# Swapping which tiles' products run on GpSimd in a selective-scan kernel, and moving its GpSimd calls, sums and side-stream steps between slots

## The chip, the cores and the metric

The kernel runs on one core of one Trainium2 chip. The metric is device time in microseconds (us) of one execution, given as the median of several. The core has TensorE (PE in the profile), VectorE (DVE), ScalarE (ACT), GpSimd (POOL) and SyncE (SP, which here issues all DMAs of the loop). Each engine works through its own queue in program order and waits on semaphores.

## The reference

Two layers on `x` of shape (8, 96, 64, 64), float32. Layer 0 is a vision state-space block with a four-direction selective scan, followed by a channel-attention convolution block; layer 1 is linear attention and an FFN with emulated float8 rounding. Cut to what matters:

```python
# layer 0, per image b of 8; C=96, DI=192 inner channels, N=16 states, 4 directions k, l = 4096 positions
xz = einsum('bhwc,ec->bhwe', layernorm(x), in_proj_w);  xw, z = split(xz)
xc = silu(depthwise_conv3x3(xw) + conv_b)
xs = [s0, s1, s0 reversed, s1 reversed]              # 8x8 windows, row- and column-first
dts, B, C = split(x_proj_w @ xs);  delta = softplus(dt_w @ dts + dt_b);  A = -exp(A_logs)
for t in range(l):                                    # for every k, channel d, state n
    h = exp(delta[t] * A) * h + (delta[t] * u[t]) * B[t]
    y[t] = sum_n h * C[t]
y = layernorm(sum of the 4 directions + D * u) * silu(z)
x1 = x * skip_scale + y @ out_proj
hcab = conv3x3(gelu(conv3x3(layernorm(x1))));  x = x1 * skip_scale2 + hcab * gate(mean(hcab))
# layer 1, on tokens t of 96 channels
t = t + linear_attention(layernorm(t));  t = t + ffn_with_float8_rounding(layernorm(t))
```

## The kernel before

**Units, tiles, slots.** The scan is cut into 256 units, written by one loop: 8 images, 4 directions, 8 chunks of 512 positions. A unit has 6 tiles (two halves `g` of the states, times three groups `j` of 64 channels); a tile is 4 slots, so a unit has 24 slots. One slot is one 128x512 scan instruction on VectorE: 64 channels times 2 states on the partitions, 512 positions along the row.

**One tile.** `inputs` (GpSimd, one 128x2048 multiply, line 1001) makes `hb` = delta*u*B for the four slots. `decays` (ScalarE, line 1129) writes exp(delta*A) of the slot two ahead into `da`, a PSUM buffer of four banks. The scan (VectorE, line 1204) runs the recurrence. Then comes the product with C: for a "banked" slot the scan writes over `da`, and VectorE multiplies `da` by C into `hb` one slot later (`product`, line 1210); otherwise the scan writes over `hb`, and GpSimd multiplies in place, four slots at once (`outputs`, line 1009). `BANKED` gives for each tile how many of its 4 slots are banked. Line 1211 or 1216 (ScalarE) copies the last column into `carry` for the next chunk. `sums` (TensorE, line 1029) adds states and halves into PSUM tiles `p`, and `gather` (ScalarE, lines 1051 and 1054) evicts them.

**The order around it** is written by hand. `plan` puts calls into the slots of a unit; the main loop emits, for each slot, the carry copies that were kept, the decay two ahead, the scan, the product of the slot before, the planned calls, and one step of the side streams. In `plan`, `u` is the unit itself, `last` the one before, `nxt` and `third` the ones after. `inputs` is put two tiles ahead into 6 buffers (`HB`). `states` loads B and C, 1 MB each for half a unit, into two buffers each; `spread` loads delta and delta*u by channel group; `scaled_input` (GpSimd, line 983) makes delta*u; `step_sizes` (ScalarE, softplus between two table loads) stands in slot 9.

**Side streams.** Generators interleave the front end of the next image (`front`) and the back end of the last (`back_end`) with the scan. A `yield n` is n slots; `yield PA` (2 slots) stands after matmuls whose result the next step reads. The steps on VectorE are at lines 302, 450, 465, 476, 545, 597, 614, 648 and 653. Each waits in VectorE's queue, between two scans, if TensorE or ScalarE is not yet done. In `gated`, ScalarE's square (line 449) and VectorE's multiply (line 450) read the same PSUM bank `dy`, in this order. `norm` is the shared layer norm, whose last step is ScalarE's `inv_std` (lines 246 and 247). `quiet` holds silu and gelu, each between two table loads (line 275), until the slot is in `CALM`. `landed` holds a step until a number of slots has passed since its DMA's request. SyncE issues every DMA of the loop; `later` gives a DMA to it three slots after the request.

Of the kernel before, what the change touches and what calls it, by code (L numbers as in the profile page):

```python
# [12 lines left out]
AF = mybir.ActivationFunctionType  # L13
# [6 lines left out]
B, C, HW = 8, 96, 64  # L20
# [10 lines left out]
SPREAD = 5  # L31
HB = 6

BANKED = ((4, 0, 4, 0, 4, 3), (4, 0, 4, 0, 4, 4))

HOLD = 3
LAND = 11
# [1 line left out]
PA = 2  # L39
# [4 lines left out]
def kernel(ctx: ExitStack, tc: tile.TileContext, a, out):  # L44
# [8 lines left out]
    nc = tc.nc  # L53
# [105 lines left out]
    def landed(*parts):  # L159
        while clock[0] < max(p.ready for p in parts):  # L160
            yield 1
# [56 lines left out]
    def windowed(ap):  # L218

        return ap.rearrange("p (w i j) -> p i w j", w=8, i=8)  # L220

    def raster(ap):
        return ap.rearrange("p (i w j) -> p i w j", i=8, w=8)

    def square(ap):
        return ap.rearrange("p (r w) -> p r w", r=8)
# [22 lines left out]
    def norm(k, srcs, sq, d):  # L249

        ps = bank(k.tag, "ctr")[:C, :]
        for i, src in enumerate(srcs):
            nc.tensor.matmul(ps, cen_c, src, start=i == 0, stop=i == len(srcs) - 1)  # L253
        yield PA
        nc.scalar.activation(sq, ps, AF.Square)
        nc.scalar.copy(d, ps)  # L256
        yield 1
        ps = bank(k.tag, "var")[:C, :]
        nc.tensor.matmul(ps, ones_c, sq, start=True, stop=True)  # L259
        yield PA  # L260
        inv_std(ps, ps)
        yield 1
        return ps

    alone = [False]
    place = [None]
    CALM = (0, 1, 16, 17)

    def quiet():

# [135 lines left out]
    def back_end(b, s):  # L406
# [8 lines left out]
        def gated(k, cs):  # L415


            def fetch_y(c):
                fetch(k.ya, s["y"][0][0:P, bass.ts(c, T)])
                fetch(k.yb, s["y"][0][P:DY, bass.ts(c, T)])  # L420

            def fetch_z(c):
                fetch(k.za, s["zd"][0:P, bass.ts(c, T)])
                fetch(k.zb, s["zd"][P:DI, bass.ts(c, T)])

            def fetch_base(c):
                fetch(k.bs, s["base"][:, bass.ts(c, T)])

            bs, r = k.bs.t[:C], k.r[:C]
            full, low, up, early = slice(0, P), slice(0, 64), slice(64, P), 0  # L430
            for n, c in enumerate(cs):
                while c not in s["done"]:
                    yield 1
                if n == 0 or early < n:
                    fetch_y(c)
                if n == 0:
                    fetch_z(c)
                    fetch_base(c)
                after = cs[n + 1] if n + 1 < len(cs) else None
                yield from landed(k.ya, k.yb, k.za, k.zb, k.bs)  # L440
                for rows, (wa, wb_), z, sq in (
                    (full, (cen_aa, cen_x), k.za.t, k.s1),
                    (up, (cen_x[:, 0:64], cen_bb), k.zb.t, k.s2[up]),
                ):
                    ps = bank(k.tag, "dy")[rows, :]
                    nc.tensor.matmul(ps, wa, k.ya.t, start=True, stop=False)  # L446
                    nc.tensor.matmul(ps, wb_, k.yb.t, start=False, stop=True)  # L447
                    yield PA
                    nc.scalar.activation(raster(sq), windowed(ps), AF.Square)
                    nc.vector.tensor_tensor(raster(z), windowed(ps), raster(z), ALU.mult)  # L450
                    yield 1
                if after in s["done"]:
                    fetch_y(after)
                    early = n + 1
                ps = bank(k.tag, "var")[:C, :]
                nc.tensor.matmul(ps, cen_x[:, 0:C], k.s1, start=True, stop=False)
                nc.tensor.matmul(ps, cen_x[up, 0:C], k.s2[up], start=False, stop=True)
                yield PA
                inv_std(r, ps, -1.0)
                yield 1  # L460
                ps = bank(k.tag, "attn")[:C, :]
                nc.tensor.matmul(ps, wy[0], k.za.t, start=True, stop=False)
                nc.tensor.matmul(ps, wy[1][up], k.zb.t, start=False, stop=True)
                yield PA
                nc.vector.tensor_tensor(r, ps, r, ALU.mult)
                if after is not None:
                    fetch_z(after)
                later(x1d[:, bass.ts(c, T)], r)
                if early == n and after in s["done"]:
                    fetch_y(after)  # L470
                    early = n + 1
                yield 1
                rs = yield from norm(k, (r, bs), k.s1[:C], k.d1[:C])
                if after is not None:
                    fetch_base(after)
                nc.vector.tensor_tensor(k.pad[0:C, :, 1 : HW + 1], square(k.d1[:C]), square(rs), ALU.mult)
                if early == n and after in s["done"]:
                    fetch_y(after)
                    early = n + 1
                later(xld[:C, 1 + 8 * c : 9 + 8 * c, :], k.pad)  # L480
                if k.solo and n == 5:
                    fetch_rows(k.im, xld, NC - 2)
                yield 1
# [42 lines left out]
        def second_conv(k, cs):  # L526
            if not k.solo:
                for p, c in zip(k.m3, cs):
                    nearer(p, c)
            for n, c in enumerate(cs):  # L530
                yield from landed(k.m3[n % 2])
                ps = bank(k.tag, "cab2")[:C, :]
                for dx in range(3):
                    nc.tensor.matmul(  # L534
                        ps, cab2_w[:, dx, :], k.m3[n % 2].t[:, :, dx : dx + HW], start=dx == 0, stop=dx == 2
                    )
                    if dx == 1:
                        yield 1
                yield PA
                if n + 2 < len(cs):  # L540
                    nearer(k.m3[n % 2], cs[n + 2])
                t = (k.s1, k.d1)[n % 2][:C]
                nc.scalar.activation(t, ps, AF.Identity, bias=cab2_b)  # L543
                yield 1
                nc.vector.tensor_reduce(totals[:, c : c + 1], t, AX.X, ALU.add)
                later(td[:, bass.ts(c, T)], t)
                if n == len(cs) - 1:
                    sources(k, cs[0])
                yield 1
# [29 lines left out]
        def attention(k, cs):  # L579

            t, x1, bs, new = k.ya.t[:C], k.za.t[:C], k.bs.t[:C], k.r[:C]
            for n, c in enumerate(cs):
                yield from landed(k.ya, k.za, k.bs)
                ps = bank(k.tag, "x2")[:C, :]
# [10 lines left out]
                rs = yield from norm(k, (new,), k.s1[:C], k.d1[:C])  # L595
# [4 lines left out]
                ps = bank(k.tag, "lnt")  # L600
# [8 lines left out]
                ps = bank(k.tag, "gram")[: C + 1, : C + 1]  # L609
                for i in range(4):  # L610
                    part = lnt[:, i * (C + 1) : (i + 1) * (C + 1)]
                    nc.tensor.matmul(ps, part, part, start=i == 0, stop=i == 3)  # L612
                yield PA
                nc.vector.tensor_tensor(gram, ps, gram, ALU.add)
                if n == len(cs) - 1:
                    normed_again(k, 0, cs[0])
# [23 lines left out]
        def feed_forward(k, cs):  # L640

            for n, c in enumerate(cs):
                t = k.t2[n % 2].t[:C]
                yield from landed(k.ln, k.t2[n % 2])
                ps = bank(k.tag, "att")[:C, :]
                nc.tensor.matmul(ps, small["qkvf"], k.ln.t, start=True, stop=True)
                yield PA
                nc.vector.scalar_tensor_tensor(t, ps, bff, t, ALU.add, ALU.add)  # L648
                if n + 1 < len(cs):
                    normed_again(k, n + 1, cs[n + 1])  # L650
# [1 line left out]
                rs = yield from norm(k, (t,), k.s1[:C], k.d1[:C])  # L652
                nc.vector.tensor_tensor(k.x8, k.d1[:C], rs, ALU.mult, saturate=False)  # L653
                yield 1
                for f in range(3):
                    ps = bank(k.tag, "ff1")
# [16 lines left out]
                ps = bank(k.tag, "ff2")[:C, :]  # L673
# [60 lines left out]
    for b in range(out.shape[0]):  # L734
# [3 lines left out]
        for order, (pair, back) in enumerate((p, k) for p in s["pairs"] for k in range(2)):  # L738
            for i in range(NC):
                u = Unit()  # L740
# [321 lines left out]
    def plan(u, last, nxt, third, fourth):  # L1062
# [3 lines left out]
        def put(slot, f, *args):  # L1066
            at[slot].append((f, args))

        if last:
            put(0, outputs, last, 5)  # L1070
            for m in range(2):
                put(m, sums, last, (3, 4), 2 + m)
            for m in range(2):
                put(3 + m, sums, last, (5,), m)
            put(3, gather, last, 0)
            put(7, states, u, 1, 1)
            put(7, gather, last, 1)
        for n in range(6):
            to = (u, n + 2) if n < 4 else (nxt, n - 4)
            if to[0]:  # L1080
                put(4 * n + 1, inputs, *to)
        if third and u.i % 2:
            put(16, scaled_input, (nxt, third))
        put(8, outputs, u, 1)
        put(16, outputs, u, 3)
        for m in range(4):
            put(13 + m, sums, u, (0, 1), m)
            if m < 2:
                put(18 + m, sums, u, (2,), m)
                put(22 + m, sums, u, (3, 4), m)  # L1090
        put(18, before, u)
        if nxt:
            put(0, spread, nxt, 0, (0, 1))
# [69 lines left out]
    for u in units:  # L1163
# [29 lines left out]
        for slot in range(24):  # L1193
            n, m = divmod(slot, G)
# [30 lines left out]
    for f in kept:  # L1225
        f()
    outputs(u, 5)
    for m in range(2):
        sums(u, (3, 4), 2 + m)
    for m in range(2):  # L1230
        sums(u, (5,), m)
    gather(u, 0)
# [79 lines left out]
```

## Time and profile before

| | us |
|---|---|
| median of 3 runs | 10794.53 (10794.46 to 10806.23) |
| the profiled execution's own time | 10803.4 |
| its span | 10801.7 |
| VectorE busy | 10015.9 (93%) |
| GpSimd busy | 9994.5 (93%) |
| TensorE busy | 8566.6 (79%) |
| ScalarE busy | 7636.8 (71%) |
| mean share of the DMA queue's packets | 84.8% |
| 6144 scans (line 1204), mean of the commonest form | 1.273 |
| 3890 products on VectorE (line 1210), mean | 0.668 |
| 1536 `inputs` (line 1001), mean | 4.546 |
| 512 full `outputs` (line 1009), mean | 4.535 |
| 384 `scaled_input` (line 983), mean | 1.29 |

Instructions of VectorE and of GpSimd overlap a little at their ends, so that the next one starts earlier than the mean duration says: on VectorE 1.18 us after a scan's start and 0.59 us after a product's, on GpSimd 4.48 us after a 128x2048 multiply's. The scans run from 179.0 to 10569.1 us of the span; before lies the setup and the front end of image 0, behind it the end of image 7. A unit takes 40.6 us on the mean.

### The profile page before, as it was taken

Reading aid. Unit: us, or ns where it says so; the run is one execution under the profiler, and the core shown is the slowest. Engines: PE = TensorE matmul, PEld = TensorE weight load, DVE = VectorE, ACT = ScalarE, POOL = GpSimd, SP = SyncE. Lnnn points to the kernel's source line nnn. Section 1 sums busy time; section 2 is a strip of 40 time slices with the busy share of each in tenths; the row PEclk is TensorE's granted clock in tenths of the full one; section 3 lists DMA queues with packets and bytes.
Section 4 is the critical chain, followed back from the end, with each engine's and each line's share of the span. In section 5 each row is a group of like instructions: output and inputs, shape, how many; then the busy total and the mean of one; then the engine's idle time right before and its main releaser. Section 6 shows DMA issues by size and latency. Waiting matters only on the chain. (4 is left out here: it accounts for less than half of the span.)

```text
span 10801.7 us, 96773 instructions
## 1 busy us (share of the span) xinstructions
PE 8566.6 (79%) x23270; PEld 2293.4 (21%) x23270; DVE 10015.9 (93%) x10848; ACT 7636.8 (71%) x14954; POOL 9994.5 (93%) x2732
## 2 busy tenths in 40 slices
PE   7777768886788868888688886888778887777677
PEld 2121112221122212222122221222212221111122
DVE  3999999999999999999999999999999999999993
ACT  4666666777677776777777777677776777666674
POOL 3999998999999999999999999999998999999991
PEclk8787778987788878888789887888878987788788
DMA  6888888988889878898888988899888988888883
GB/s 148 205 206 212 200 211 210 228 222 202 216 212 225 224 195 222 210 230 216 201 215 211 237 209 204 212 219 232 201 214 213 220 228 201 204 204 210 210 211 93
DMA packets 1095373, 2253.23 MB, mean 209 GB/s; under 512 B 435993, under 2 KB 436698, under 8 KB 963731
## 3 DMA queue, kind: packets, MB, share of 16 engines
q1 hardware_dynamic: 1094803, 2247.05, 84.8%
q8 instruction: 185, 3.03, 0.1%
q14 instruction: 385, 3.15, 0.1%
HBM read 1507.14 MB, written 336.69 MB: 171 GB/s over the span
## 5 line engine op out<-in xcount | busy, mean ns | idle before, releaser
L1001 POOL TENSOR_TENSOR hb<-b,du 128x2048 f32<-128x2048 f32 x1536 | 6949.6, 4546 | 23.9 <-PE p L1029 16.8
L1129 ACT ACTIVATE da<-delta,w_a_logs 128x512 f32<-128x512 f32 x6144 | 4147.6, 689 | 496.6 <-DVE hb L1204 400.4
L1029 PE MATMUL p<-hb,halves 128*64 128x512 f32 x12288 | 3786.8, 706 | 791.0 <-POOL hb L1009 630.7
L1204 DVE TENSOR_TENSOR_SCAN da<-da,carry,hb 128x512 f32<-128x512 f32 x3385 | 4258.5, 1273 | 129.5 <-ACT carry L1211 55.9
L1009 POOL TENSOR_TENSOR hb<-hb,c 128x2048 f32<-128x2048 f32 (+1 forms) x718 | 2587.7, 3604 | 395.5 <-ACT carry L1216 373.6
L1210 DVE TENSOR_TENSOR hb<-da,c 128x512 f32<-128x512 f32 x3890 | 2599.3, 668 | 1.8 <-DMA c<-xd 0.8
L1204 DVE TENSOR_TENSOR_SCAN hb<-da,carry,hb 128x512 f32<-128x512 f32 x1991 | 2451.4, 1264 | 65.2 <-ACT carry L1211 49.2
L1211 ACT COPY carry<-da 128x1 f32<-128x1 f32 x3890 | 609.9, 157 | 1784.0 <-DVE hb L1210 1775.1
L1029 PEld LDWEIGHTS p<-hb,halves 128*64 128x64 f32 x12288 | 907.4, 157 | 3551.9 <-issue 1979.6
L313 PE MATMUL conv<-f0im,taps 97*128 97x512 f32 (+1 forms) x2088 | 890.2, 675 | 45.9 <-ACT f0pre L369 42.4
L275 ACT ACT_TABLE_LOAD x705 | 904.5, 1283 | 13.7 <-PEq L1301 0.8
L1204 DVE TENSOR_TENSOR_SCAN da<-da,hb 128x512 f32<-128x512 f32 x505 | 605.3, 1214 | 56.4 <-POOL hb L1001 54.0
L962 PE MATMUL dt<-dts,dt_w 7*128 7x512 f32 (+1 forms) x1024 | 484.9, 740 | 157.0 <-ACT yt L1054 69.1
L983 POOL TENSOR_TENSOR ua<-nat,ua 128x512 f32<-128x512 f32 x256 | 329.8, 1288 | 167.0 <-DMA ub<-u 157.9
L313 PEld LDWEIGHTS conv<-f0im,taps 97*128 97x128 f32 (+1 forms) x2088 | 257.9, 177 | 629.3 <-issue 532.2
L1216 ACT COPY carry<-hb 128x4 f32<-128x4 f32 (+1 forms) x718 | 140.1, 195 | 323.5 <-DVE hb L1204 318.5
L1204 DVE TENSOR_TENSOR_SCAN hb<-da,hb 128x512 f32<-128x512 f32 x263 | 308.1, 1205 | 3.4 <-ACT carry L1211 2.1
L259 PE MATMUL var<-f1e,ones_c 96*96 96x512 f32 x350 | 215.8, 701 | 119.5 <-ACT f1e L256 63.4
L253 PE MATMUL ctr<-f1e,cen_c 96*96 96x512 f32 x402 | 226.7, 672 | 105.0 <-DVE f1e L648 43.1
L657 PE MATMUL ff<-f1x,q_w 96*128 96x512 fp8e5 x174 | 83.0, 477 | 254.2 <-DVE f1x L653 150.9
L497 PE MATMUL cab<-f1im,cab_w 97*32 97x512 f32 x1044 | 261.5, 615 | 13.4 <-DMA f1im<-xld 7.2
L534 PE MATMUL cab<-f1m,cab_w 96*96 96x512 f32 x348 | 213.8, 735 | 54.4 <-ACT f1e L543 25.8
(427 smaller groups left out, 7118.3 us busy)
## 6 DMA issues: line engine op xcount, KB each, us to landing
b<-xd SPq DMA_DIRECT2D x1024, 512.0 KB
c<-xd SPq DMA_DIRECT2D x1024, 512.0 KB
delta<-nat SPq DMA_DIRECT2D x1536, 128.0 KB
du<-ua SPq DMA_DIRECT2D x1024, 128.0 KB
y<-yt SPq DMA_DIRECT2D x512, 256.0 KB
u<-y SPq DMA_DIRECT2D x384, 256.0 KB
ua<-u SPq DMA_DIRECT2D x256, 256.0 KB
du<-ub SPq DMA_DIRECT2D x512, 128.0 KB
```

What stands on the lines that cost most here:

```text
L275: nc.scalar.preload_act_table_set(name)
L313: nc.tensor.matmul(ps, taps[:, t, lo : lo + n], im[:, r0 + dy : r0 + dy + 8, dx : dx + HW], start=t == 0, stop=t == 8,)
L497: nc.tensor.matmul(ps[at : at + 32, :], cab1_w[:, t, :], k.im.t[:, 8 * q + dy : 8 * q + dy + 8, dx : dx + HW], start=t == 0, stop=t == 8, ...
L962: nc.tensor.matmul(to, dt_w.rearrange("r j d -> r (j d)")[32 * w.k : 32 * w.k + R + 1, d], w.dts, start=True, stop=True)
L983: nc.gpsimd.tensor_tensor(x, nat, x, ALU.mult)
L1001: nc.gpsimd.tensor_tensor(hb, u.bc[0, g], u.du[j].unsqueeze(1).to_broadcast([P, G, T]), ALU.mult)
L1009: nc.gpsimd.tensor_tensor(hb, hb, u.bc[1, TILES[n][0]][:, lo:, :], ALU.mult)
L1029: nc.tensor.matmul(ps, halves, u.hb[n][:, i, :], start=TILES[n][0] == 0 and m == 0, stop=False, skip_group_check=True)
L1129: nc.scalar.activation(da[q], u.delta[j], AF.Exp, scale=a_neg[:, u.k, j, g * G + m : g * G + m + 1])
L1204: nc.vector.tensor_tensor_scan(dd if banked else x, dd, x, 0.0 if u.start else col, ALU.mult, ALU.add)
L1210: nc.vector.tensor_tensor(x, d, c, ALU.mult)
L1211: kept.append(lambda: nc.scalar.copy(col, d[:, at : at + 1]))
```

## The change

Six edits at once; no arithmetic is added or dropped.

1. `BANKED` swaps the first two tiles: tile 0's products go from VectorE to GpSimd, tile 1's from GpSimd to VectorE.
2. In `plan`, `inputs` goes from slots 1, 5, 9, 13, 17, 21 to 0, 4, 9, 12, 16, 20. The full `outputs` in slot 8 (tile 1) becomes one in slot 4 (tile 0).
3. `sums` of tiles 0 and 1 go from slots 13-16 to 12-15, of tile 2 from 18-19 to 17-18, of tiles 3 and 4 from 22, 23, 0, 1 to 23, 0, 1, 2; tile 5's stay in 3 and 4. `gather` goes from 3 and 7 to 4 and 6.
4. Side streams: one slot more ahead of VectorE's steps at lines 465, 545, 614 and 648, and after `inv_std` in `norm` (ahead of 302, 476, 597 and 653).
5. In `gated`, VectorE's multiply comes first and ScalarE's square of the same bank a slot later; the waits for z and base move to where they are used, and `fetch_base` is requested inside `norm`.
6. `CALM`, where silu and gelu may stand, goes from (0, 1, 16, 17) to (4, 5, 16, 17, 18, 19).

```diff
-BANKED = ((4, 0, 4, 0, 4, 3), (4, 0, 4, 0, 4, 4))
+BANKED = ((0, 4, 4, 0, 4, 3), (0, 4, 4, 0, 4, 4))
@@ norm
         inv_std(ps, ps)
-        yield 1
+        yield 2
@@
-    CALM = (0, 1, 16, 17)
+    CALM = (4, 5, 16, 17, 18, 19)
@@ gated
-                yield from landed(k.ya, k.yb, k.za, k.zb, k.bs)
+                yield from landed(k.ya, k.yb)
...
                     yield PA
-                    nc.scalar.activation(raster(sq), windowed(ps), AF.Square)
+                    yield from landed(k.za, k.zb)
                     nc.vector.tensor_tensor(raster(z), windowed(ps), raster(z), ALU.mult)
                     yield 1
+                    nc.scalar.activation(raster(sq), windowed(ps), AF.Square)
+                yield 1
...
-                yield PA
+                yield PA + 1
                 nc.vector.tensor_tensor(r, ps, r, ALU.mult)
...
-                rs = yield from norm(k, (r, bs), k.s1[:C], k.d1[:C])
+                yield from landed(k.bs)
+                steps = norm(k, (r, bs), k.s1[:C], k.d1[:C])
+                yield next(steps)
                 if after is not None:
                     fetch_base(after)
+                rs = yield from steps
@@ second_conv, ahead of the tensor_reduce
-                yield 1
+                yield 2
@@ attention, ahead of gram; feed_forward, ahead of the first VectorE step
-                yield PA
+                yield PA + 1
@@ plan
-            for m in range(2):
-                put(m, sums, last, (3, 4), 2 + m)
+            for m in range(3):
+                put(m, sums, last, (3, 4), 1 + m)
             for m in range(2):
                 put(3 + m, sums, last, (5,), m)
-            put(3, gather, last, 0)
+            put(4, gather, last, 0)
+            put(6, gather, last, 1)
             put(7, states, u, 1, 1)
-            put(7, gather, last, 1)
-        for n in range(6):
+        for n, slot in enumerate((0, 4, 9, 12, 16, 20)):
             to = (u, n + 2) if n < 4 else (nxt, n - 4)
             if to[0]:
-                put(4 * n + 1, inputs, *to)
+                put(slot, inputs, *to)
...
-        put(8, outputs, u, 1)
+        put(4, outputs, u, 0)
         put(16, outputs, u, 3)
         for m in range(4):
-            put(13 + m, sums, u, (0, 1), m)
-            if m < 2:
-                put(18 + m, sums, u, (2,), m)
-                put(22 + m, sums, u, (3, 4), m)
+            put(12 + m, sums, u, (0, 1), m)
+        for m in range(2):
+            put(17 + m, sums, u, (2,), m)
+        put(23, sums, u, (3, 4), 0)
```

More of the change, by code (lines that the diff above doesn't have):

```diff
@@ L646, in feed_forward @@
                 nc.tensor.matmul(ps, small["qkvf"], k.ln.t, start=True, stop=True)
-                yield PA
+                yield PA + 1
                 nc.vector.scalar_tensor_tensor(t, ps, bff, t, ALU.add, ALU.add)
@@ L1227 @@
     outputs(u, 5)
-    for m in range(2):
-        sums(u, (3, 4), 2 + m)
+    for m in range(1, 4):
+        sums(u, (3, 4), m)
     for m in range(2):
```

## The prediction

> **What bounds the kernel now.** I read the page's busy shares first, then busy time by image, then who waits on VectorE and on GpSimd in one image, then the timeline of a unit.
>
> ```profile
> PE 8566.6 (79%) x23270; PEld 2293.4 (21%) x23270; DVE 10015.9 (93%) x10848; ACT 7636.8 (71%) x14954; POOL 9994.5 (93%) x2732
> ```
>
> Two engines are equally full, so neither alone is the bound. By image (start:end, length, then busy of PE, PEld, DVE, ACT, POOL, each with its count), for images 0, 2 and 7; images 1 and 3 to 6 look like 2:
>
> ```profile
> 179.00:1438.20 1259.20, 925.66 (x2400) 239.16 (x2402) 1200.97 (x1265) 847.41 (x1667) 1235.60 (x329) 0.79 0.86 206
> 2745.30:4051.80 1306.50, 1062.19 (x2910) 280.79 (x2909) 1247.63 (x1344) 955.72 (x1874) 1248.88 (x340) 0.84 0.87 215
> 9281.00:10569.10 1288.10, 942.77 (x2552) 251.52 (x2549) 1255.21 (x1356) 885.66 (x1787) 1239.57 (x335) 0.81 0.84 205
> ```
>
> A unit of image 2 takes 1306.5 / 32 = 40.83 us and holds 38.99 us of VectorE work and 39.03 of GpSimd work. No reordering brings it under 39.03: at most 1.8 us a unit, 58 an image. Image 0 takes 39.35 a unit and is GpSimd's already (38.61). What VectorE waited for in image 2 (us, times, longest):
>
> ```profile
> DVE da L1204 <- ACT carry L1211: 9.6, 5, 3.2
> DVE da L1204 <- POOL hb L1001: 8.8, 9, 2.2
> DVE f1e L465 <- PE attn L463: 8.1, 5, 4.2
> DVE hb L1204 <- ACT carry L1211: 7.5, 10, 2.3
> DVE f1x L450 <- ACT f1e L449: 7.0, 3, 4.4
> DVE f1pre L450 <- ACT f1pre L449: 5.0, 5, 3.1
> DVE f1x L653 <- ACT var L247: 3.6, 4, 1.8
> DVE f1ln L597 <- ACT var L247: 2.9, 4, 1.4
> DVE f1pad L476 <- ACT var L247: 1.7, 2, 1.5
> ```
>
> Of 58.9 us, side steps (465, 450, 653, 597, 476 and small ones) hold 29, scans that wait for ScalarE 21 (these two rows and 4 us of decays), scans that wait for GpSimd 9. GpSimd's timeline (start, length) shows its side:
>
> ```profile
> 4646.94 4.52 POOL L1009 TENSOR_TENSOR hb<-hb,c 128x2048 f32<-128x2048 f32 x1 [1.74 <-ACT carry L1216]
> 4651.41 4.53 POOL L1001 TENSOR_TENSOR hb<-b,du 128x2048 f32<-128x2048 f32 x1
> 4655.90 1.26 POOL L983 TENSOR_TENSOR ua<-nat,ua 128x512 f32<-128x512 f32 x1
> 4657.13 4.51 POOL L1001 TENSOR_TENSOR hb<-b,du 128x2048 f32<-128x2048 f32 x1
> 4661.59 4.52 POOL L1009 TENSOR_TENSOR hb<-hb,c 128x2048 f32<-128x2048 f32 x1
> 4666.07 9.01 POOL L1001 TENSOR_TENSOR hb<-b,du 128x2048 f32<-128x2048 f32 x2
> ```
>
> Once a unit it stops at tile 1's `outputs`, until that tile's last scan (1.74 us here, 51.8 in image 2); everything behind runs back to back. So GpSimd loses its spare time at the wrong place: `inputs` for the next unit's tile 0, sixth in the queue from there, ends only 2.0 us ahead of its scan on the mean, 0.03 in the worst tenth.
>
> **GpSimd's order (edits 1 and 2).** Calls and durations stay; 9,994 us stays 9,994. Take scan 0 as zero. Before, the scans of slots 4, 8, 12, 16, 20 start at 6.9, 12.7, 20.2, 26.0, 33.0 and the next unit at 40.6. Tile 0 without products shortens its four slots by 3 x 0.59 = 1.8, so slot 4 comes at 5.1; from slot 8 on all is as before. GpSimd after, at 4.48 a full call and 1.23 a small one: tile 5's row of the last unit 0.5 to 1.7, `inputs` 2 to 6.2, `inputs` 3 to 10.7, `outputs` 0 to 15.2 (ready at 5.1: no stop), `inputs` 4 to 19.7, 5 to 24.2, small 25.4, next 0 to 29.9, half a small 30.5, `outputs` 3 to 35.0, next 1 to 39.5. Ahead of their scans by 6.5, 9.5, 6.3, 8.8, 10.7 and 6.2 us, where the trace has 4.4, 7.4, 2.9, 4.2, 2.0 and 4.5. The 8.8 us row should nearly go; I keep 3 for units that come late: gain 6 an image.
> New waits here: next tile 0 at 25.4 needs its buffer's sums, now slots 12 to 15. TensorE starts the last of them at 24.5 in the trace, 1.5 before slot 16; one slot earlier is 23.2, done by 24.3. It also needs B, whose DMA is issued at 13.4 (median) and by the trace's semaphore updates lands at 22.2, in the worst tenth 25.7, at most about 28.4. A wait to 28.4 costs 3 us of GpSimd's spare and leaves next tile 1 3 us. Behind it in GpSimd's queue stand delta*u of the third group, `outputs` 3 and next tile 1. Taken: 0; bounds 0 to 1 us a unit.
> SyncE's queue is passed too: in every second unit the small call in slot 16 now follows next tile 0, and SyncE waits for it before it issues delta*u of the third group and then B of the second half. In the trace these land at least 6.1 and 3.0 us (median 10.5 to 11.9, and 9.1) ahead of `inputs` 2 and 3; 4.48 less leaves 1.6 and, at the worst, a 1.5 us wait of `inputs` 3, which is 9.5 early. Cost 0.
>
> **Side steps (edits 4 and 5).** One slot is at least 1.18 us, 1.77 with a product. Taking 1.5 off each wait: over images 1 to 6, 465 goes from 49.2 to 17.0 us, 653 from 22.6 to 1.6, 597 and 476 from 28.3 to 0. For 450 VectorE now waits for TensorE itself: if TensorE ends as now, the first one waits 29.9 us (45.0 before), the second 0 (30.3); but its matmuls now stand behind ScalarE's square, about 1.5 us later, which gives back some 18. So 75 becomes 48. Together 179 becomes about 68: 18 us an image. Bounds: 8 (the waits go along with late engines) to 27. The longer streams cost nothing at the end: before, the front end's last step comes 78 slots ahead of the point where it must be drained (of 772 an image), after it 31. ScalarE's square then waits for VectorE, a decay queued behind it; multiply and next square are a slot apart, so 0, at most 0.7 x 16 an image.
>
> **ScalarE (edits 3 and 6).** This is where the change can lose. Softplus in slot 9: the decay before it needs the bank of slot 7, now freed by a product, so the table load starts 0.9 after scan 9's start rather than 0.4 at best. In images 1 to 6 it already starts at 0.9 or later in half the units, held by side steps. With 0.9 as a floor the waits at slot 12 grow by 8 us in 192 units, with 0.5 added everywhere by 52: 1.5 to 9 an image, 3 taken. Silu and gelu:
>
> ```profile
> 4622.17 1.28 ACT L275 ACT_TABLE_LOAD   x1
> 4623.47 1.48 ACT L321 ACTIVATE f0pre<-f0pre 128x1536 f32<-128x1536 f32 x1
> 4624.97 1.28 ACT L275 ACT_TABLE_LOAD   x1
> ```
>
> One silu holds ScalarE 4.1 us and its decays with it: about 1 us of VectorE when it runs at slot 16, 0.6 at 17, 0.1 to 0.7 at 1, 2.5 to 4 where another step collides; 11 an image in all. The built program has eight silus and four gelus an image before and after; after, four silus at 16 (one with a gelu in the same slot, as before), three at 4, one at 5. At 1 us plus collisions that is 15: 4 lost, bounds -5 to 10. The later sums and `gather` leave TensorE 2.4 us instead of 3.5 between the last sum and its eviction in tiles 0 to 4: 3 lost, 0 to 8.
> A rule against edit 6: the Trainium skill, "ScalarE: Activation LUTs", section "What ACT_TABLE_LOAD costs", puts a drain of 1380 ns on every 1283 ns load. The rows show 1283 and the silu 20 ns later, so the trace disagrees and decides. By that figure softplus would hold ScalarE 2.8 us longer, end after scan 12 is due in every unit, and its later start would count in full: an estimate of 0.5 x 32 = 16 lost an image where I have 3.
>
> **Sum.** An image like 2: 6 + 18 - 3 - 4 - 3 = 14, times six 84. Image 7 (33 idle, 24 of it side steps) 8. Image 0 waits for GpSimd, which itself was idle 23.6 us, 11.8 of it at `outputs` 1: 5. Setup and tail: four streams go in step there and wait for each other's engines, not for slots: 0, 10 either way. 97 in all: 10803.4 - 97 = 10706 in the profiled execution's terms, 9 less in those of the median (10803.4 against 10794.5): 10700 rounded. A measurement of this kernel can tell 0.2% (22 us) from no change.
>
> **Rivals.**
> *The waits vanish altogether* (12%): both engines close to 39.4 a unit. For: every `inputs` gains 2 us or more. Against: 21 us an image of ScalarE waits that no edit touches. 6 x 46 + 25 is 300 at the most; 200 lies between that and my 97: 10595.
> *The side waits only change their releaser* (9%): 450 and 465 wait for TensorE as they did for ScalarE, gain 8; with 6 from GpSimd and 10 lost, 4 an image: 10780, no change.
> *ScalarE at slot 9* (13%, slower): tables, now behind a full run of products and side steps, end after scan 12 is due. 56 of 192 units wait there now, 0.74 each. All else gains 97 + 3 x 7 = 118, so it decides at 118 / 224 units, 0.5 us a unit; at 1 us a unit the kernel ends at 10794 + 224 - 118 = 10900.
> *B lands too late for next tile 0* (8%, slower): GpSimd's spare is 1.8 us a unit now and 1.4 after. A wait of 2.5 each unit puts the excess of 1.1 on the end: 246, less 97: 10943. It decides at a wait of 1.4 + 97 / 224 = 1.8 us a unit. Against: the landings above; for: DMA at 0.87 busy, which any speed-up raises.
>
> **The numbers.** Forecast 58%. Faster by over 0.2%: 58 + 12 = 0.70; within 0.2%: 0.09; slower: 0.21. The bounds of my terms give 0 to 210 us of gain, the range takes half of each other case: 10560 to 10870.
>
> **What would show it.** Right: GpSimd's wait at `outputs` from carry 1216 gone from full calls, VectorE's wait for `inputs` under 30 us (96 now), 465, 653, 597 and 476 together under 60 us in the whole run, 450 still waiting, now for TensorE; images 1 to 6 near 1292. Wrong: scans waiting for ScalarE over 30 us an image (slot 9 or the tables), GpSimd rows waiting for b or for `p`, or TensorE waiting longer for `outputs` 3 at slot 23.

## The result, and the profile after

The changed kernel takes 10975.03 us (median of 4 runs, 10966.33 to 10976.56) beside 10796.89 for the kernel before on the same chip: a ratio of 1.0162, 95% interval 1.0144 to 1.0179. It is 178 us slower, where 97 us of gain were forecast. The profiled execution took 10976.56, its span 10974.8.

Busy time is first, from the page:

```profile
PE 8299.0 (76%) x23270; PEld 2267.1 (21%) x23270; DVE 10090.2 (92%) x10848; ACT 7658.1 (70%) x14954; POOL 9991.5 (91%) x2732
```

GpSimd's work is the same to 3 us, as it should be. VectorE has 74 us more in the same number of instructions: something lasts longer. The rest is waiting. The window of image 2 (start:end, length, busy of PE, PEld, DVE, ACT, POOL, then clock and DMA):

```profile
2779.70:4115.50 1335.80, 1033.69 (x2908) 279.65 (x2908) 1258.41 (x1345) 958.54 (x1874) 1249.28 (x340) 0.83 0.86 211
```

Images 0 and 7 grew by 11 and 12 us. Image 2 grew from 1306.5 to 1335.8 instead of shrinking to 1292. Of the 29.3 us, 10.8 are VectorE's longer busy time and 18.5 its longer idle time. The main rows of what it waited for in image 2 (us in all, times, longest):

```profile
DVE da L1209 <- ACT da L1134: 33.6, 20, 5.4
DVE hb L1209 <- ACT da L1134: 7.1, 8, 2.3
DVE f1pre L450 <- PE dy L447: 4.4, 1, 4.4
DVE f1x L450 <- PE dy L447: 4.2, 2, 3.0
DVE f1e L467 <- PE attn L465: 4.1, 1, 4.1
```

Scans that wait for decays (line 1134 now) went from 4 us to 41; side steps (450, 467 and what is left of the others) from 29 to 17. The lines have moved: scan 1209, `inputs` 1006, `outputs` 1014, `sums` 1034, `gather` 1056 and 1059.

Why would ScalarE be late? The whole run's waits name the engines one step further back. Before, TensorE's wait for `outputs` was

```profile
PE p L1029 <- POOL hb L1009: 630.7, 206, 9.4
```

and `gather` waited 23 us for TensorE. After:

```profile
PE p L1034 <- POOL hb L1014: 1254.7, 232, 14.2
ACT yt L1059 <- PE p L1039: 194.9, 113, 5.4
ACT yt L1059 <- PE p L1043: 99.1, 84, 3.8
ACT yt L1056 <- PE p L1039: 74.7, 38, 4.4
ACT yt L1056 <- PE p L1043: 41.7, 43, 2.6
POOL hb L1006 <- issue: 310.8, 84, 8.2
```

TensorE waits 1255 us for `outputs`, `gather` on ScalarE waits 410 us for TensorE, and GpSimd's `inputs` waits 311 us for something the page calls issue. One passage of image 2 holds the whole chain; four pieces of the timeline, for GpSimd, TensorE, ScalarE and VectorE (start, length, instruction, idle time before it and its releaser):

```profile
3157.96 4.53 POOL L1006 TENSOR_TENSOR hb<-b,du 128x2048 f32<-128x2048 f32 x1 [4.13 <-issue]
3162.44 4.51 POOL L1014 TENSOR_TENSOR hb<-hb,c 128x2048 f32<-128x2048 f32 x1
```

```profile
3167.00 5.86 PE L1034 MATMUL p<-hb,halves 128*64 128x512 f32 x16 [5.73 <-POOL hb L1014]
```

```profile
3173.95 1.11 ACT L1056 COPY yt<-p 128x512 f32<-128x512 f32 x1 [3.60 <-PE p L1039]
3175.08 1.28 ACT L275 ACT_TABLE_LOAD   x1
3176.37 1.48 ACT L321 ACTIVATE f0pre<-f0pre 128x1536 f32<-128x1536 f32 x1
3177.87 1.28 ACT L275 ACT_TABLE_LOAD   x1
```

```profile
3179.89 1.29 DVE L1209 TENSOR_TENSOR_SCAN da<-da,carry,hb 128x512 f32<-128x512 f32 x1 [3.61 <-ACT da L1134]
```

The next unit's tile 0 (`inputs`, 3157.96) starts late and `outputs` 3 stands behind it. TensorE takes up `sums` of tiles 3 and 4 at 3167.00, 0.05 us after `outputs` 3 ends, having waited 5.73. `gather` of the last unit waits 3.60 for those sums. A silu is queued behind `gather`, the decays behind the silu, and a scan waits 3.61.

Figures worked out from starts and ends in the traces say how near to the edge this is. In images 1 to 6 after, `outputs` 3 ends 0.6 us ahead of the start of slot 23 on the mean and behind it in 43% of the units; before, it ends 3.0 us ahead of slot 22, the slot of its first reader then, and is late in 3%. And the next unit's tile 0 starts at 29.5 on the mean of all units, where I had 25.4. In images 1 to 6 it waits in 117 of 192 units, and in 99 of them it starts about 0.13 us after the end of TensorE's last sum of tiles 0 and 1. So nearly all of the wait for "issue" (280 of the 311 us) is a wait for these sums. That last sum starts at 27.1 on the mean of all units, where I had 23.2. A late TensorE explains little of this: the same sum starts at 27.8 in the trace of before, and at 26.5 in the run below that exchanges the two GpSimd calls. My figure was too early.

The longer busy time is one instruction. Groups of lines, before first, after second (busy, mean ns, idle time before it):

```profile
L572 DVE TENSOR_SCALAR dgate<-ident,gate 96x96 f32<-96x96 f32 x8 | 32.0, 4002 | 0.3
```

```profile
L577 DVE TENSOR_SCALAR dgate<-ident,gate 96x96 f32<-96x96 f32 x8 | 98.0, 12249 | 0.3
```

It makes the diagonal gate of the channel attention, once an image, and no edit touches it. After, at one of them, VectorE and then GpSimd:

```profile
2060.79 14.06 DVE L577 TENSOR_SCALAR dgate<-ident,gate 96x96 f32<-96x96 f32 x1
```

```profile
2060.16 1.26 POOL L988 TENSOR_TENSOR ua<-nat,ua 128x512 f32<-128x512 f32 x1
2061.38 4.50 POOL L1006 TENSOR_TENSOR hb<-b,du 128x2048 f32<-128x2048 f32 x1
2065.84 4.49 POOL L1014 TENSOR_TENSOR hb<-hb,c 128x2048 f32<-128x2048 f32 x1
2070.30 4.49 POOL L1006 TENSOR_TENSOR hb<-b,du 128x2048 f32<-128x2048 f32 x1
```

It ends at 2074.85, 0.06 us after a short call and three full ones that follow it without a gap. The eighth one, behind the last scan with GpSimd idle, takes 0.27. Before, at the same place, VectorE and then GpSimd:

```profile
2122.95 4.35 DVE L572 TENSOR_SCALAR dgate<-ident,gate 96x96 f32<-96x96 f32 x1
```

```profile
2122.73 4.51 POOL L1001 TENSOR_TENSOR hb<-b,du 128x2048 f32<-128x2048 f32 x1
2128.80 4.52 POOL L1009 TENSOR_TENSOR hb<-hb,c 128x2048 f32<-128x2048 f32 x1 [1.56 <-ACT carry L1216]
```

There the multiply ran from 2122.95 to 2127.30 and ended 0.06 us behind one call, where GpSimd then stopped for 1.56 us at `outputs` of tile 1. Edits 1 and 2 take these stops away.

### The profile page after: what moved, and what is told of

Read it like the earlier page. It is cut to its first block, busy times and chain, and to the rows that moved or that the text cites. A ratio compares the mean times of both kernels' runs of the same rounds, so it can differ in the third digit from the quotient of the medians.

```text
span 10974.8 us, 96818 instructions
## 1 busy us (share of the span) xinstructions
PE 8299.0 (76%) x23270; PEld 2267.1 (21%) x23270; DVE 10090.2 (92%) x10848; ACT 7658.1 (70%) x14954; POOL 9991.5 (91%) x2732
## 5 line engine op out<-in xcount | busy, mean ns | idle before, releaser
L1034 PE MATMUL p<-hb,halves 128*64 128x512 f32 x12288 | 3729.5, 723 | 1379.8 <-POOL hb L1014 1254.7
L313 PE MATMUL conv<-f0im,taps 97*128 97x512 f32 (+1 forms) x2088 | 867.5, 649 | 57.5 <-ACT carry L1216 33.2
L967 PE MATMUL dt<-dts,dt_w 7*128 7x512 f32 (+1 forms) x1024 | 428.3, 637 | 22.9 <-ACT carry L1216 11.3
L1059 ACT COPY yt<-p 128x512 f32<-128x512 f32 x368 | 214.4, 583 | 297.3 <-PE p L1039 194.9
L1056 ACT COPY yt<-p 128x512 f32<-128x512 f32 x144 | 158.3, 1100 | 117.6 <-PE p L1039 74.7
```

The source lines that it names most:

```text
L313: nc.tensor.matmul(ps, taps[:, t, lo : lo + n], im[:, r0 + dy : r0 + dy + 8, dx : dx + HW], start=t == 0, stop=t == 8,)
L967: nc.tensor.matmul(to, dt_w.rearrange("r j d -> r (j d)")[32 * w.k : 32 * w.k + R + 1, d], w.dts, start=True, stop=True)
L1034: nc.tensor.matmul(ps, halves, u.hb[n][:, i, :], start=TILES[n][0] == 0 and m == 0, stop=False, skip_group_check=True)
```

## The experiments

Theory: two causes, `outputs` 3 behind the next unit's tile 0, and the gate multiply held by GpSimd; the side steps gain what was forecast. Rivals: the tables (softplus in slot 9, silu and gelu in the new `CALM`), and side steps that gain nothing. All ratios are to the kernel before, run beside on the same chip (10797 to 10800 us).

**The gate multiply.** After, with this multiply on ScalarE:

```diff
-            nc.vector.tensor_scalar(dgate, ident[:C, :C], gate, None, ALU.mult)
+            yield 1
+            nc.scalar.activation(dgate, ident[:C, :C], AF.Identity, scale=gate)
             yield 1
```

> The changed kernel with one instruction per image moved: the 96x96 multiply that makes dgate runs on ScalarE instead of VectorE. In the traces it takes 4.35 us before and 14.05 us after, seven times, beside GpSimd calls that follow each other without a stop, and 0.27 us where GpSimd is idle. Theory (VectorE is held until GpSimd pauses, and this time lies on the path that sets the end): 7 x 14 = 98 us of VectorE less, of which part was hidden by later waits; 10,875 to 10,915 us. Rival (VectorE catches up within the image because GpSimd sets the pace): within 15 us of the changed kernel's 10,975.

10856.09, ratio 1.0053 (1.0038 to 1.0068): 119 us less than after, more than the 98 of its own busy time on VectorE; TensorE, which waited 96 us for it ahead of line 591 in after, waits 3 here.

The same edit on the kernel before:

> The kernel before with dgate made on ScalarE and nothing else. There it takes 4.36 us seven times. Theory: 20 to 40 us less, 10,755 to 10,780. Rival (the wait is hidden behind GpSimd): within 10 us of 10,797.

10752.97, ratio 0.9959 (0.9945 to 0.9974): 47 us. Its price was there before the change, and the change more than doubled it.

**The order of GpSimd's two calls.** After, with `outputs` 3 ahead of the next unit's tile 0 in slot 16:

```diff
+        put(16, outputs, u, 3)
         for n, slot in enumerate((0, 4, 9, 12, 16, 20)):
...
-        put(16, outputs, u, 3)
```

> The changed kernel with two GpSimd calls exchanged in slot 16: outputs of tile 3 ahead of inputs of the next unit's tile 0. Theory (a loop: next tile 0 waits for TensorE's sums of slots 12 to 15; outputs 3 behind it comes late; TensorE stops at the sums of slot 23, gather on ScalarE stops, decays come late): TensorE's wait for outputs (1255 us on matmuls) falls below 500, ScalarE's wait in gather (410 us) below 150, scans waiting for ScalarE fall by a third or more, 10,860 to 10,920 us. Rival (the table loads in slots 4 and 5 are the cause by themselves): those waits of TensorE fall, but the time stays within 25 us of 10,975.

10793.49, ratio 0.9996 (0.9987 to 1.0005): 181 us back (the edit puts `outputs` 3 ahead of the short call of slot 16 too). TensorE's wait:

```profile
PE p L1034 <- POOL hb L1014: 680.3, 169, 10.2
```

`outputs` 3 now ends 6.5 us ahead of slot 23 and is never late; the gate multiply still takes 11.6 us.

The other way round, the kernel before with this order alone:

```diff
-        put(16, outputs, u, 3)
+        put(17, outputs, u, 3)
```

(`inputs` of tile 0 was put in slot 17 already, and is issued first there.)

> Before, with nothing changed but outputs 3 put in slot 17 behind the inputs of the next unit's tile 0, not in slot 16 ahead of them; the sums of tiles 3 and 4 stay in slots 22 and 23. Theory (outputs 3 that ends late holds TensorE at slot 22, then gather, then ScalarE's decays): 10850 to 10980, TensorE's wait for outputs over 1000 us. Rival (the order hurts only together with the other moves, and earlier inputs of tile 0, 2.0 us ahead of its scan before, gain): 10760 to 10800.

11020.87, ratio 1.0208 (1.0193 to 1.0223): 221 us lost by one call that stands one place later, more than the whole change loses. The waits of TensorE and of two groups on VectorE:

```profile
PE p L1029 <- POOL hb L1009: 1402.2, 263, 15.0
DVE hb L1204 <- ACT carry L1211: 136.7, 84, 5.5
DVE f1x L450 <- ACT f1e L449: 107.0, 34, 5.6
```

`outputs` 3 ends 2.0 us behind the start of slot 22 and is late in 84% of the units. This decides for the order. It also says what more of TensorE's wait costs: with 1402 us of it instead of 631, scans wait 239 us in images 1 to 6 instead of 174, and side steps 302 instead of 180.

**The two halves of the change.** The kernel before with edits 4 and 5 alone, and with edits 1, 2, 3 and 6 alone:

> The kernel before with the side-stream edits alone (one slot more ahead of VectorE's steps, the two readers of dy exchanged, the later fetches); tiles, plan and CALM as before. Theory (these edits do what the prediction said, the loss is all in plan and CALM): side steps' waits on VectorE fall from 177 us in images 1 to 6 to about 80, time 10,700 to 10,745 us. Rival (the exchanged readers and longer streams hold TensorE and ScalarE up): 10,780 us or more.

10713.93, ratio 0.9921 (0.9905 to 0.9938): 85 us gained. Images 1 to 6 take 1293.4 us on the mean, 13.7 less than before; the side steps' waits in all six fall from 177 us to 33. The time does not fall by as much: scans of slot 12, which stand behind softplus, wait 88 us for ScalarE instead of 41, and the gate multiply takes 10.0 us instead of 4.0, because the streams reach it at another place in GpSimd's queue.

> The other half alone: tiles, plan and CALM as changed, side streams as before. Theory (the loss is here): 10,980 to 11,060 us, slower than the whole change, with TensorE's wait for outputs and the late decays as in the changed kernel. Rival (the two halves only lose together): under 10,850 us.

10967.12, ratio 1.0156 (1.0141 to 1.0171): the plan loses 168 us without the side steps, and with a gate multiply of 2.9 us. In the whole change this multiply takes 12.2, 75 us more over eight images, which is of the size of what the side steps gain; so the two kernels are level.

Edits 4 and 5 with the gate multiply on ScalarE:

> The kernel before with the side-stream edits and with dgate made on ScalarE. In the run of the side-stream edits alone dgate takes 11.6 us on the mean of eight. Theory (two independent gains): 7 x 13 = 91 us of VectorE less, most of it on the path: 10,620 to 10,650 us. Rival (without that stop of VectorE the next wait takes its place): above 10,690.

10630.44, ratio 0.9846 (0.9832 to 0.9861). This is the fastest of all versions here. (The 11.6 us of the expectation are the mean in the run with `outputs` 3 first; in the side steps alone it is 10.0.)

**The tables.** After with the old `CALM`, and after with softplus a slot earlier:

```diff
-    CALM = (4, 5, 16, 17, 18, 19)
+    CALM = (0, 1, 16, 17)
```

> The changed kernel with CALM as before (0, 1, 16, 17), so silu and gelu leave slots 4 and 5. Theory A (table loads at 4 and 5 stand right behind the blocked gather and cost about 90 us): 10,890 to 10,930. Theory B (the blocked gather is the root; table loads at 0 and 1 stand ahead of it and among five slots without a product, and cost as much): within 30 us of 10,975, with the waits moved to slots 2 to 5.

10837.64, ratio 1.0034 (1.0025 to 1.0044): 137 us less than after (median of ten, 10812.71 to 10851.51), and a trap. In the execution profiled, of 10817 us, the gate multiply met the end of a short GpSimd call:

```profile
L577 DVE TENSOR_SCALAR dgate<-ident,gate 96x96 f32<-96x96 f32 x8 | 3.2, 402 | 0.3
```

So the old `CALM` was tried again with the gate multiply on ScalarE, where it takes 0.36 to 0.38 us each time:

> After with the gate multiply on ScalarE and the old CALM slots (0, 1, 16, 17). The gate multiply cannot be held by GpSimd here, so what differs from the run with the gate alone (10856) is CALM alone. Theory (CALM small; the 137 us of the run with the old CALM alone were the gate multiply): 10820 to 10850. Rival (CALM of ScalarE is a main cause, 137 by itself): 10720, with scans waiting for decays under 200 us in images 1 to 6.

10832.43, ratio 1.0030 (1.0018 to 1.0042): 24 us less than with the gate alone. So `CALM` costs 24, hardly more than the 22 that a measurement can tell from nothing; the other 113 of the 137 go to the gate multiply, whose own time was 95 us shorter in the execution profiled.

```diff
-                put(8, step_sums, (nxt, third))
-            put(9, step_sizes)
+                put(7, step_sums, (nxt, third))
+            put(8, step_sizes)
```

> The changed kernel with softplus in slot 8 instead of 9, and the matmuls of the pair ahead of it in slot 7. Theory (the prediction's rival: softplus ends after scan 12 is due): the 86 us that scans of slot 12 wait for ScalarE in images 1 to 6 fall below 30, and the kernel by 50 to 100 us, 10,875 to 10,925. Rival (ScalarE is late all through, the wait only moves to slots 9 to 11): within 25 us of 10,975.

10978.89, ratio 1.0169 (1.0154 to 1.0184): no difference to after. The 86 us of waits at slot 12 in images 1 to 6 went to slot 11, where there are 154.

**Putting it together.** After with the gate on ScalarE and `outputs` 3 first; then with the old `CALM` too:

> After with the gate multiply on ScalarE and outputs 3 ahead of the next unit's tile 0. Theory (two separate causes, GpSimd's order worth 181 and the gate multiply 46 to 119): 10675 to 10750. Rival (both use up the same spare time, only one counts): 10790 and no better than the order alone.

10699.91, ratio 0.9909 (0.9892 to 0.9925): the two causes add up (119 us for the gate multiply and then 156 for the order, or 181 for the order and then 94). That this run lands on the forecast of 10,700 is luck: the kernel before pays 47 us for the gate multiply too, so the rest of the change gains 53 us here and not 97.

> As the run with the gate and outputs 3, and CALM old too. Theory (order, gate multiply and CALM are the whole loss, the swap of tiles itself gives at most the 6 us an image that I forecast): 10590 to 10650, level with the side steps with the gate on ScalarE (10630). Rival (the swap of BANKED, the earlier calls or the later sums lose something of their own): 10680 or more.

10675.38, ratio 0.9886 (0.9871 to 0.9901). The theory falls here by 45 us: this kernel differs from that of 10630.44 by nothing but the swap of tiles, the slots of `inputs` and those of sums and `gather`, and should be level with it.

**The 45 us.** Two guesses, each undoing one part: the old slots of sums and `gather`, the old slots of `inputs`:

> As the run with outputs 3 first, the gate multiply on ScalarE and the old CALM (10675), with the sums of tiles 2, 3 and 4 and both gathers back in the slots of before (18 and 19; 22, 23, 0, 1; 3 and 7). Theory (the later sums and gather lose the 45 us, since gather waits for TensorE): 10620 to 10645. Rival (the swap of tiles 0 and 1 itself loses it): within 15 us of 10675.

```diff
-            put(17 + m, sums, u, (2,), m)
-        put(23, sums, u, (3, 4), 0)
+            put(18 + m, sums, u, (2,), m)
+            put(22 + m, sums, u, (3, 4), m)
...
-            put(4, gather, last, 0)
-            put(6, gather, last, 1)
+            put(3, gather, last, 0)
+            put(7, gather, last, 1)
```

10672.68, ratio 0.9882 (0.9865 to 0.9898): no difference. (The sums of tiles 0 and 1 keep their new slots.)

> As the run at 10675, with inputs in slots 1, 5, 9, 13, 17 and 21 again, so that in slots 4 and 5 outputs of tile 0 stands ahead of the inputs of tile 3. Theory (sums and gather lose the 45 us, not the calls of inputs): within 15 us of 10675. Rival (issuing inputs ahead of outputs delays outputs and what follows it): 10620 to 10650.

```diff
-        for n, slot in enumerate((0, 4, 9, 12, 16, 20)):
+        for n, slot in enumerate((1, 5, 9, 13, 17, 21)):
```

10688.50, ratio 0.9902 (0.9887 to 0.9917): no gain either. So the swap of tiles 0 and 1 is left, with the slots of its `outputs` and sums, as far as undoing one part at a time can tell; no run has the swap alone. In the trace of 10675.38 the scans of images 1 to 6 wait 26 us less for GpSimd than in that of 10630.44, and 70 us more for decays. In slots 2 to 5 decays hold 72 us instead of 7, most of it (59 us) within 9 us of a table load of silu or gelu, and tile 0, in slots 0 to 3, has no products now. A last guess puts silu over tile 1, in the kernel with the swap and in the one without:

```diff
-    CALM = (0, 1, 16, 17)
+    CALM = (4, 5, 16, 17)
```

> As the run with outputs 3 first and the gate multiply on ScalarE, with CALM (4, 5, 16, 17): silu and gelu over tile 1, whose slots have products after the swap. Theory (the swap loses 45 us because silu in slots 0 and 1 holds the decays of a tile without products): decay waits of slots 2 to 5 fall from 72 us to under 15 in images 1 to 6, and 10600 to 10645. Rival (the decays stand behind silu wherever it is; they come late in slots 7 and 8 then): 10670 to 10700.

10701.67, ratio 0.9911 (0.9897 to 0.9926).

> The side steps with the gate multiply on ScalarE (10630), with CALM (4, 5, 16, 17) and no swap: silu over tile 1, which has no products here. Theory (silu over a tile without products costs 45 us): 10660 to 10700, with late decays in slots 6 to 9. Rival (the place of silu does not matter): 10620 to 10640.

10747.77, ratio 0.9953 (0.9937 to 0.9970). Without the swap slots 4 and 5 cost 117 us, with it 26: silu's place and the swap do belong together. But the decays that were late in slots 2 to 5 are late in slot 7 instead (100 us in images 1 to 6 with the swap, 102 without), and the swap stays behind. Of these, 88 and 101 us come within 9 us of a table load of silu or gelu, as the rival of the run with the swap had it: decays stand behind silu wherever it is. Why tile 1's products don't spare them is open, and with it the cause of the 45 us.

The measured kernels make one chain of steps between the two (its sum is right by construction): 10797 for the kernel before, -44 for the gate multiply on ScalarE (47 beside the kernel before on the same chip), -123 for the side steps, +45 for swap, `inputs`, sums and `gather`, +25 for `CALM`, +156 for the order, +119 for the gate multiply back on VectorE: 10975.

## Why the prediction was wrong, step by step

**GpSimd's order** failed. "Next 0 to 29.9 ... `outputs` 3 to 35.0" was a row of durations laid end to end; measured, `outputs` 3 ends at 39.1 on the mean of all units. The step read the price of a wait as "GpSimd's spare" and asked what is late next only among `inputs`. The reader of `outputs` 3 stands in the prediction's last line alone, among the signs of being wrong, and no term prices it. It is TensorE, whose queue holds the next sums, `gather`'s sources and the side streams' matmuls behind that sum. "Taken: 0; bounds 0 to 1 us a unit" cost 0.6 us a unit by one pair of runs (156 us over 256 units) and 0.7 by the other (181). The bound held it, and the choice within it was wrong: the row to look at was TensorE's 631 us of waiting for `outputs`, which already stood in the trace of before.

**The trigger** was not the one I weighed. I looked at B's landing; tile 0 waits 1.5 us a unit on the mean, and nearly all of it for sums. "TensorE starts the last of them at 24.5" misread the trace of before: 24.5 is the start of the last matmul of the second of the four slots' sums. That of the fourth is 27.8, and it ends at 28.4, so a call moved up to 25.4 had to wait even with a slot taken off. "One slot earlier is 23.2" then took a slot for a time: the move gained 0.6 us, to 27.1.

**"Calls and durations stay"** held for GpSimd. For VectorE the sum had no term at all, and that is the second step that failed: the removed stop at `outputs` 1 was the gap in which the gate multiply ended. Moving this multiply away gains 119 us in the changed kernel and 47 in the kernel before. The rival on B priced the side of slower kernels at 10943, near the result, by another mechanism.

**The swap** was to gain 6 us an image. Its GpSimd side is seen, scans wait 26 us less for GpSimd over six images, 4.3 each. By what is left after the experiments it loses 45 in all: the sum had no term for later decays, 70 us here. That a tile without products gives ScalarE less time for them is the likely reason and not shown, since moving silu over tile 1 did not bring the 45 back.

**Side steps** were right: 18 us an image were forecast, and images 1 to 6 gain 13.7 each with these edits alone and 18.4 where the gate multiply is on ScalarE on both sides. That 450 now waits for TensorE was right too, but in after TensorE is late, and its wait, with 467, is 72 us in images 1 to 6 instead of 65.

**ScalarE**: `CALM` at 4 us an image and later sums at 3 were forecast as 24 and 18 lost over images 1 to 6; over the whole run `CALM` measured 24 and 25, the sums nothing. Softplus in slot 9, a rival at 13%, measured nothing either. The 16 us an image that the Trainium skill's drain behind table loads would have made of it ("ScalarE: Activation LUTs", "What ACT_TABLE_LOAD costs") are not seen: in the passage above the silu follows its load by 10 ns.

Of the signs, the wait at full `outputs` went and 450 changed its releaser. VectorE's wait for `inputs` went from 102 to 77, not under 30 (the row of 96 fell to 59, but the first scans of tile 0 have moved to the row beside it, 18 instead of 6). The steps at 465, 653, 597 and 476 wait 114 us in the whole run, not under 60. All three wrong signs came: scans wait 50 us an image for ScalarE (298 in images 1 to 6), TensorE waits twice as long for `outputs`, and GpSimd waits for `p`, 69 us by name (17 before) and most of the 311 under "issue".

The Trainium skill, "SBUF — State Buffer", section "Who interferes with whom", says that `tensor_scalar` can run in a mode that takes a port pair which VectorE shares with GpSimd, and that whoever issues first holds the pair for the whole instruction while the other fully blocks. The rows agree with the blocking (0.27 us alone, 14.06 beside GpSimd, ending 0.06 us behind a call), but show it across more than one GpSimd instruction. That the shared pair is the reason is the page's word; no run here shows the port, or the mode.

## What to carry to other kernels

Before moving a call in one engine's queue, list who reads what stands behind it, and how far ahead of its reader it ends now: 3.0 us was all there was, and one call of 4.5 us took it. A queue that is made to run without a stop can hold another engine's small instruction over several of its calls, 14 us here; look for short instructions whose mean is many times their shortest. And when one edit seems to explain more than the rest together, look whether an unrelated instruction changed its duration in that run.

## What I had not expected of the hardware

The gate multiply (96x96) took 0.27 us with GpSimd idle, 0.45 at the end of a short call, 4.35 beside one full call, and 14.06 across the end of a short call and three full ones. It did not get through at the three boundaries between those four calls, which overlap by 0.03 to 0.04 us. What decides at which boundary it gets through isn't settled: in the run with the old `CALM` alone it did behind a short call, though the next call overlaps that one by 0.05 us.

A wait of TensorE costs more than its length. In after, in the 38 groups of 16 or more matmul records of sums that follow a wait of 5 to 10 us and run without a gap, pairs of records start 0.85 us apart for about 4.3 us and then 0.43 (medians; before shows the same, with 28 groups). So a held sum comes late and then runs at half speed for these first microseconds.
